# Two row tiles first, and later list rounds among the edge groups, in the head of a graph layer

## The chip, the core and the metric

The kernel runs on one core of one Trainium2 chip. The time is the device time of one execution in microseconds (us). The five engines of the core are called PE (matrix products and transposes), DVE (vector work), ACT (activations and copies), POOL (here it issues the indirect gathers) and SP (it issues the plain transfers). Each engine works through its own instructions in a fixed order; an instruction waits on semaphores for what it needs from others, and all that stands behind it on its engine waits too.

## The reference, cut to what matters

One layer takes `x` (6250 rows of 256 numbers), 200000 edges `src`, `dst` sorted by `dst`, and weights. It adds three parts: a graph attention, a linear attention over all rows, and a feed-forward part with four experts that is steered by a second, smaller graph attention over 131072 other edges.

```python
xn = _layernorm(x)
# graph attention, 4 heads of 64
z = jnp.einsum('ni,hid->nhd', xn, W)
es, ed = (z * a_src).sum(-1), (z * a_dst).sum(-1)
e = leaky(es[src] + ed[dst], 0.01)
alpha = softmax of e over the edges of one dst
gnn = segment_sum(alpha[:, :, None] * z[src], dst)
# linear attention over all rows
mix = layernorm_gamma(softmax(q) @ (softmax_over_rows(k).T @ v) @ Wout)
x = x + gnn + mix
x = x + ffn(_layernorm(x))      # a second attention over other edges picks experts
```

The change is in what stands ahead of the first attention's sums over edges: the first norm, `z`, the products with the two attention vectors, and the lists of edges.

## The kernel before

**Tiles.** The rows are cut into NT = 49 tiles of 128 (the last has 106). The first attention works on "chunks" of 128 edges of one destination tile: 33 chunks for each tile and 28 for the last, 1612 in all, taken in groups of G1 = 8.

**The head: project.** `load_x` (an SP transfer) brings XB = 7 tiles of x into one of three buffers `xa`. `project_x` treats such a batch: on DVE the statistics (`bn_stats`, `bn_aggr`, lines 519 and 520), on ACT a square root and on DVE five small steps that refine it (lines 125 to 135, called `ln_q`, `ln_r`); then for each tile the normalised rows `xn` (DVE, line 525), two transposes on PE into `ln_tp` (line 145), a copy to `xy` on ACT (line 529), two products `zp` on PE (line 532), and three copies out of `zp`: z to `zt` (ACT, line 534), the source term to the end of `zt` (DVE, line 537) and both terms to `es_all` (ACT, line 538). SP stores `zt` to the table `ztab` in memory (line 539). `zp` and `ln_tp` have two buffers each, `zt` has eight. The statistics of a batch are held back until the third tile of the batch before is normalised (`tc.issue_after`).

**The head: attention vectors.** `wz` holds the weights (256 columns) and eight more columns, the weights times the attention vectors (lines 576 and 577 on DVE, in four pairs of product and reduction). Since `zp` is a product with all 264 columns, these stand ahead of the first batch.

**The head: order of the edges.** A flag says whether `dst` is unsorted (`down`, `d`, `flag`, lines 590 to 597). Every engine reads it and branches (lines 599 to 602); the sorted data skip the branch. Behind it, lines 609 to 683 find where each destination tile begins in the sorted edges (`fd` in the room of `kx`, line 622; `lt`, `cf`, the product `cp`, `sel`, the product `row`, `less`, `start_k`, the product `ip`), and end with the addresses `at` (line 681). POOL then fetches with 26 indirect transfers (line 689) the sources `sr` and destinations `dr` of every chunk, two for each of BS = 13 blocks of 128 chunks.

**The head: lists.** `lists(b0)` makes four blocks ready for the edge stage: destinations less the tile's base (`fl`, line 700), clamped sources (`fs`, line 704), a bf16 copy (line 705) that SP stores as `rows_1` (line 706), then transposes on PE into `e_tp` (line 712) and copies on DVE to `src_c` and `dl_c` (line 713). `src_c` holds the row numbers that the edge stage gathers by. There are four rounds. Each is held back by `tc.issue_after` until a late tile is through: tiles NT - 17, NT - 10, NT - 3 and NT - 2.

```python
for b0, t in zip(range(0, BS, 4), (NT - 17, NT - 10, NT - 3, NT - 2)):
    with tc.issue_after(zmm[t].ins), tc.issue_after(xnv[t].ins), tc.issue_after(zst[t].ins):
        lists(b0)
```

`S.activation(warm, r[:, 0:1], AF.Exp)` reads the last batch's root; it is there to bring ACT's exponential table in.

**Behind the head.** Line 197 takes a maximum over `es_all` (`f_m`), then POOL begins the gathers of `ztab` by `src_c` (line 774), eight for each of 202 groups; three buffers `gt` hold them. A group's weights need the gathered source terms (`src_d`, line 208, ACT lines 209 and 210), destination terms (`ed`, line 813, from `pw3`) and one-hot matrices (lines 798 and 807); DVE weighs the rows (line 833) and PE adds them up (line 842). The linear attention's steps (`k_max` and others, whose running maximum is `kmax`, line 871) and the sort of the other edges are dealt out among the groups. A second edge stage of the same kind follows (line 1303 on POOL), with the experts' products beside it.

**What sets the order.** Instructions are not issued in the order of the text: a scheduler orders each engine's instructions when the program is built, by what it takes to be ready, within the data dependencies and the `issue_after` marks. A tile's buffer that takes the place of an older one waits for the older one's readers.

Of the kernel before, what the change touches and what calls it, by code (L numbers as in the profile page):

```python
# [9 lines left out]
F32 = mybir.dt.float32  # L10
# [10 lines left out]
P = 128  # L21
N = 6250
D = 256
# [33 lines left out]
def rows(t):  # L57
    return min(P, N - t * P)
# [3 lines left out]
def gps_layer(ctx: ExitStack, tc: tile.TileContext, a: dict, out: bass.AP):  # L62
# [425 lines left out]
    wz = room_2[:, : 2 * 264].rearrange("p (j f) -> p j f", j=2)  # L488
    es_all = room_2[:, 2 * 264 : 2 * 264 + NT * 8].rearrange("p (t f) -> p t f", f=8)
    XB = 7  # L490
    with tc.tile_pool(name="a_x", bufs=1) as ax, tc.tile_pool(name="a_w", bufs=3) as aw, tc.tile_pool(
        name="a_p", bufs=2, space=PSUM
    ) as aps:
# [5 lines left out]
        def load_x(t0):  # L499
            ts_ = range(t0, min(t0 + XB, NT))  # L500
            xa = aw.tile([P, XB, D], F32, name="xa")
            whole = [t for t in ts_ if rows(t) == P]
            SP.dma_start(
                xa[:, : len(whole)],
                a["x"][t0 * P : (t0 + len(whole)) * P, :].rearrange("(t p) d -> p t d", p=P),
            )
            for t in ts_:
                if rows(t) < P:
                    SP.dma_start(xa[: rows(t), t - t0], a["x"][t * P : N, :])
            xas[t0] = xa  # L510

        def project_x(t0):
            ts_ = range(t0, min(t0 + XB, NT))
# [8 lines left out]
            for t in ts_:  # L522
                n, n0 = rows(t), t * P
                xn = aw.tile([P, D], F32, name="xn")
                xnv[t] = V.tensor_scalar(
                    xn[:n], xa[:n, t - t0], mv[:n, t, 0:1], r[:n, t - t0 : t - t0 + 1], op0=OP.subtract, op1=OP.mult
                )
                tp = transposed(aps, xn, n, "ln_tp")
# [5 lines left out]
                S.copy(  # L534
                    zt[:n, :ZW].rearrange("p (h d) -> p h d", h=4)[:, :, 0:64], zp[:n, 0:256].rearrange("p (h d) -> p h d", h=4)
                )
                V.tensor_copy(zt[:n, ZW:], zp[:n, 256:260])
                S.copy(es_all[:n, t, :], zp[:n, 256:264])
                zst[t] = SP.dma_start(ztab[n0 : n0 + n, :], zt[:n])
            return r  # L540
# [20 lines left out]
        with tc.tile_pool(name="e_w", bufs=1) as w:  # L561
# [32 lines left out]
            with tc.tile_pool(name="fl_p", bufs=1, space=PSUM) as ps:  # L594
                d2 = ps.tile([1, 1], F32, name="d2")
                T.matmul(d2, d1, ones[:, 0:1], start=True, stop=True)
                V.tensor_scalar(flag, d2, 1.0, None, op0=OP.min)
            project_x(XB)
            unordered = nc.values_load(
                flag[0:1, 0:1], min_val=0, max_val=1, skip_runtime_bounds_check_because="a count of 0s and 1s, at most 1"  # L600
            )
# [1 line left out]
                with tc.tile_pool(name="ord_w", bufs=1) as ow:  # L603
                    order_edges(ow, bs, bd)

            load_x(3 * XB)
            project_x(2 * XB)
            for ord_, b_ in ((d_ord, bd), (s_ord, bs)):
                SP.dma_start(ord_.rearrange("(b r j) o -> r b (j o)", r=P, j=P), b_)
            with tc.tile_pool(name="e_l", bufs=1) as w, tc.tile_pool(name="e_p", bufs=1, space=PSUM) as ps:  # L610
# [68 lines left out]
                V.tensor_add(at_f, at_f, ip[:, :, 0])  # L679
                at = w.tile([P, BS], I32, name="at")  # L680
                V.tensor_scalar(at, at_f, float(B1 * P * P - P), None, op0=OP.min)
# [12 lines left out]
                fl = take(BS, P, F32)  # L694
                fb = tk.bitcast(BF16)[:, : BS * P].rearrange("p (b j) -> p b j", b=BS)

                def lists(b0):
                    bb = slice(b0, min(b0 + 4, BS))
                    nb = bb.stop - b0
                    V.tensor_tensor(  # L700
                        fl[:, bb], dr[:, bb], base[:, bb].unsqueeze(2).to_broadcast([P, nb, P]), op=OP.subtract
                    )

                    V.tensor_scalar(fs[:, bb], sr[:, bb], float(N - 1), None, op0=OP.min)
                    V.tensor_copy(fb[:, bb], fl[:, bb])
                    SP.dma_start(
                        rows_1[b0 * P * P : bb.stop * P * P, :].rearrange("(b s j) o -> s b (j o)", s=P, j=P), fb[:, bb]
                    )
                    for f, c_ in ((fs, src_c), (fl, dl_c)):
                        tp = ps.tile([P, 4, P], F32, name="e_tp")  # L710
                        for b in range(nb):
                            T.transpose(tp[:, b], f[:, b0 + b], ident)
                        V.tensor_copy(c_[:, b0 * P : (b0 + nb) * P], tp[:, :nb].rearrange("p b j -> p (b j)"))

                for t0 in range(3 * XB, NT, XB):
                    if t0 + XB < NT:
                        load_x(t0 + XB)
                    r = project_x(t0)
# [299 lines left out]
    with tc.tile_pool(name="g1_w", bufs=2) as w, tc.tile_pool(name="g1_g", bufs=3) as gp, tc.tile_pool(  # L1018
# [46 lines left out]
        for g in range(NGR):  # L1065
# [689 lines left out]
```

## Time and profile before

| what | before |
|---|---|
| median of 3 runs | 3260.65 us (3256.18 to 3268.05) |
| the profiled execution's own time | 3258.8 us |
| its span, first to last instruction | 3257.0 us |
| mean granted clock of PE | 0.857 |
| busy: PE, DVE, ACT, POOL | 2334.0, 2439.4, 480.6, 2344.4 us |
| `at` ready (line 681) | at 63.87 us |
| last tile's copy out of `zp` (line 537) | at 108.99 us |
| first gather of the edge stage (line 774) | at 114.90 us |
| last gather of that stage | at 2175.6 us |
| gathers of the second stage (line 1303) | 2200.4 to 3202.7 us |

Times in the trace are microseconds from the first instruction. A row of the timeline gives the start, the duration, the engine, the line, the operation, what it writes and reads, and in brackets how long the engine had been idle before it and what ended that. A name such as `src` or `dl` in a row is the buffer that a tile lies in, without its number: `wz` and `es_all` lie in `src_2`, so rows that write them say `src`; `lists` and `fd` work in the room of `kx`.

### The profile page before, as it was taken

To read this page: it belongs to the slowest core of one execution; us is meant where nothing else is said; L and a number is where in the kernel's file an instruction comes from. 1 tells how busy PE (TensorE), PEld (TensorE's weight loads), DVE (VectorE), ACT (ScalarE), POOL (GpSimd) and SP (SyncE) were. 2 spreads that over 40 slices of the span, in tenths; PEclk is the share of its full clock that TensorE was granted. 3 is DMA by queue.
4 is the path that set the end of the run, shared out by engine and by line. 5 is a ranking of instruction groups with operands and counts; after the bars stand their busy time and mean duration, and the time that the engine had idled before them with its cause. 6 is when DMAs were issued, how large, how long until landed. Compare 5 with 4: busy or idle time off the path is not lost. (4 is left out here: it accounts for less than half of the span.)

```text
span 3257.0 us, 36396 instructions
## 1 busy us (share of the span) xinstructions
PE 2334.0 (72%) x10899; PEld 1699.4 (52%) x10900; DVE 2439.4 (75%) x6337; ACT 480.6 (15%) x1266; POOL 2344.4 (72%) x2436
## 2 busy tenths in 40 slices
PE   7677778865666574665665666658777877888888
PEld 5555666654455453554544545445455545555555
DVE  7587767788888887886886878667676766777775
ACT  3200111111111111111111111013111111111111
POOL 2577777777777777777777777757777777777772
PEclk9788888987888887787888878779998998999989
DMA  6544444445555555555555555534223223333321
GB/s 202 155 135 135 136 129 127 137 134 145 150 139 151 143 137 140 138 141 143 141 153 142 147 140 142 138 92 101 61 62 78 60 57 92 81 76 80 78 51 37
DMA packets 248273, 384.90 MB, mean 118 GB/s; under 512 B 73414, under 2 KB 156246, under 8 KB 248057
## 3 DMA queue, kind: packets, MB, share of 16 engines
q0 software_dynamic: 103296, 230.96, 28.9%
q1 hardware_dynamic: 142857, 150.87, 15.4%
q8 instruction: 91, 1.49, 0.2%
q14 instruction: 125, 1.02, 0.1%
q10 hardware_dynamic: 1904, 0.56, 0.1%
HBM read 345.44 MB, written 36.74 MB: 117 GB/s over the span
## 5 line engine op out<-in xcount | busy, mean ns | idle before, releaser
L774 POOL DMA_INDIRECT gt<-ztab,src_c x1612 | 1551.2, 962 | 528.1 <-issue 424.7
L842 PE MATMUL ag<-gt,oh 128*128 128x260 f32 x3224 | 980.1, 461 | 348.3 <-DVE gt L833 347.0
L842 PEld LDWEIGHTS ag<-gt,oh 128*128 128x128 f32 x3224 | 732.6, 234 | 516.0 <-DVE gt L833 375.9
L1303 POOL DMA_INDIRECT gt<-htab,src x784 | 764.6, 975 | 262.5 <-issue 210.0
L833 DVE TENSOR_TENSOR gt<-gt,dv 128x1040 f32<-128x1040 f32 x403 | 488.8, 1223 | 0.2 <-DVE src L409 0.2
L1424 PE MATMUL yo<-w,hT 128*128 128x256 f32 x1568 | 420.8, 411 | 15.8 <-DVE ys L1467 15.8
L1404 PE MATMUL hp<-xy,w 128*128 128x512 f32 (+1 forms) x832 | 407.2, 612 | 8.6 <-ACT hT L1409 4.5
L1424 PEld LDWEIGHTS yo<-w,hT 128*128 128x128 f32 x1568 | 303.5, 203 | 96.1 <-issue 26.3
L208 DVE TENSOR_TENSOR src_d<-gt,most 128x32 f32<-128x32 f32 x204 | 38.6, 189 | 355.6 <-DMA gt<-ztab,src_c 344.3
L868 PE MATMUL m<-wqkv,xy 128*128 128x256 f32 (+1 forms) x784 | 235.8, 436 | 88.8 <-DVE kmax L879 43.6
L798 DVE TENSOR_TENSOR oh<-dv,dl_c 128x1024 f32<-128x1024 f32 x202 | 243.9, 1207 | 0.0
L868 PEld LDWEIGHTS m<-wqkv,xy 128*128 128x128 f32 (+1 forms) x784 | 160.7, 215 | 125.1 <-DVE kmax L879 49.6
L1404 PEld LDWEIGHTS hp<-xy,w 128*128 128x128 f32 x832 | 159.9, 205 | 112.4 <-issue 98.3
L1409 ACT ACTIVATE hT<-hp,b 128x512 f32<-128x512 f32 (+1 forms) x208 | 132.8, 660 | 517.6 <-PE hp L1404 294.9
L209 ACT ACTIVATE src_f<-src_d,shift_c 128x32 f32<-128x32 f32 x202 | 64.9, 321 | 928.2 <-DVE src_d L208 836.3
L1361 DVE TENSOR_TENSOR pr<-dv,gt 128x64 f32<-128x64 f32 x98 | 21.9, 223 | 227.0 <-DMA gt<-htab,src 219.5
L1385 PE MATMUL ag<-mq,oh 128*128 128x120 bf16 x784 | 66.3, 236 | 150.4 <-DVE mq L1377 141.0
L813 PE MATMUL ed<-pw,ohT 128*128 128x24 bf16 x1612 | 72.1, 175 | 125.5 <-DVE ohT L807 111.1
L373 DVE MAX8 src<-dl 128x8 f32<-128x1024 f32 x128 | 156.0, 1219 | 0.4 <-issue 0.4
L1385 PEld LDWEIGHTS <-oh 128*128 128x128 bf16 x784 | 51.6, 107 | 198.5 <-DVE mq L1377 176.6
L375 DVE MATCH_REPLACE8 dl<-src,dl 128x1024 f32<-128x1024 f32 x127 | 153.4, 1208 | 0.0
L813 PEld LDWEIGHTS <-ohT 128*128 128x128 bf16 x1612 | 64.0, 98 | 165.4 <-DVE ohT L807 134.3
(350 smaller groups left out, 2695.0 us busy)
## 6 DMA issues: line engine op xcount, KB each, us to landing
br<-rows SPq DMA_DIRECT2D x299, 256.0 KB
gt<-ztab,src_c POOLq DMA_INDIRECT x1612
gt<-htab,src POOLq DMA_INDIRECT x784
early<-ys SPq DMA_DIRECT2D x24, 512.0 KB
ys<-early SPq DMA_DIRECT2D x24, 512.0 KB
ztab<-zt SPq DMA_DIRECT2D x48, 132.0 KB
row<-in_x_dram SPq DMA_DIRECT2D x48, 128.0 KB
out_dram<-ys SPq DMA_DIRECT2D x48, 128.0 KB
```

Source lines behind the costliest of these rows:

```text
L373: V.max(out=srtf[:, 8 * i : 8 * i + 8], in_=keyf)
L375: V.match_replace(out=keyf, in_to_replace=srtf[:, 8 * i : 8 * i + 8], in_values=keyf, imm_value=0.0)
L774: G.indirect_dma_start(out=self.gt[:, c, :], out_offset=None, in_=ztab[:, :], in_offset=bass.IndirectOffsetOnAxis(ap=self.idx[:, c : c + 1 ...
L798: V.tensor_tensor(self.oh[:, :n], self.dv[:, None, :P].to_broadcast([P, n, P]), self.dl[:, :, None].to_broadcast([P, n, P]), op=OP.is_equal,)
L813: T.matmul(self.ed[:, c, :], self.ohT[:, c * P : (c + 1) * P], pw3[:, ds(self.tiles[c], 1), :].rearrange("p a b -> p (a b)"), start=True, ...
L833: V.tensor_mul(gz, gz, self.wp[:, c0:c1].unsqueeze(3).to_broadcast([P, c1 - c0, 4, 65]))
L842: T.matmul(sums[t], self.oh[:, c], self.gt[:, c, 0:ZW], start=(s0 + c == 0 or chunk_tile[s0 + c - 1] != t), stop=last,)
L868: T.matmul(out_, xy[:, t, j, :n], wqkv[:, j, c0 : c0 + D], start=(j == 0), stop=(j == 1))
L1303: G.indirect_dma_start(out=self.gt[:, c, : tab.shape[1]], out_offset=None, in_=tab[:, :], in_offset=bass.IndirectOffsetOnAxis(ap=self.idx[ ...
L1404: T.matmul(hp[:, :m], wts[e][0][:, c, j * P : (j + 1) * P], xy[:, t0 : t0 + nt, c] if m == nt * P else xy[:, t0, c, :m], start=(c == 0), s ...
L1409: S.activation(h[:, :m], hp[:, :m], AF.Gelu, bias=b1[:, e, j : j + 1])
L1424: T.matmul(yo[:n], hT[j][:, o : o + n], wts[e][1][:, j, :], start=(j == 0 and e < EARLY), stop=(j == 3))
```

## The change

The first seven tiles become two batches, of two and of five tiles; the 42 others stay in batches of seven. The two first loads go out together ahead of the others. The products with the attention vectors stand behind the normalised rows of the first two tiles, and are done for both halves of the weights at once: two products and two reductions of twice the size. The load of a later batch is asked for one batch ahead, as before. `base` moves to a pool that lives through the edge stage. Only round 0 of `lists` stays in the head; rounds 1, 2 and 3 are called in the edge loop after groups 2, 6 and 10, with `e_tp` in the edge stage's own psum pool (one buffer), and without `issue_after` marks. `warm` reads the constant `eps`.

```diff
+    batches = [range(0, 2), range(2, XB)] + [range(t0, min(t0 + XB, NT)) for t0 in range(XB, NT, XB)]
...
-        def project_x(t0):
-            ts_ = range(t0, min(t0 + XB, NT))
-            xa = xas[t0]
-            with tc.issue_after(xnv[t0 - XB + 2].ins) if t0 else nullcontext():
+        def project_x(i, weights=None):
+            ts_, t0 = batches[i], batches[i][0]
+            xa = xas[i]
+            with tc.issue_after(xnv[batches[i - 1][0] + min(2, len(batches[i - 1]) - 1)].ins) if i else nullcontext():
...
+            ready = {}
+            if weights:
+                ready = {t: normal(t) for t in ts_}
+                weights()
+            for t in ts_:
+                n, n0 = rows(t), t * P
+                xn = ready[t] if weights else normal(t)
...
         load_x(0)
+        load_x(1)
...
-            load_x(XB)
             load_blocks(bs, a["src"], E1)
-            load_x(2 * XB)
-            for s in range(2):
-                for j in range(2):
-                    V.tensor_mul(prs[:, j], wz[:, j, 0:256], avs[:, s])
+            load_x(2)
+
+            def weights():
+                for s in range(2):
+                    V.tensor_mul(prs, wz[:, :, 0:256], avs[:, None, s].to_broadcast([P, 2, D]))
                     V.tensor_reduce(
-                        wz[:, j, 256 + 4 * s : 260 + 4 * s], prs[:, j].rearrange("p (h d) -> p h d", h=4), AX.X, OP.add
+                        wz[:, :, 256 + 4 * s : 260 + 4 * s], prs.rearrange("p j (h d) -> p j h d", h=4), AX.X, OP.add
                     )
-            project_x(0)
-            with tc.issue_after(xnv[2].ins):
+
+            project_x(0, weights)
+            load_x(3)
+            project_x(1)
+            with tc.issue_after(xnv[4].ins):
...
-            project_x(XB)
+            project_x(2)
...
-            load_x(3 * XB)
-            project_x(2 * XB)
+            load_x(4)
+            project_x(3)
...
-                base = w.tile([P, BS], F32, name="base")
+                base = ek.tile([P, BS], F32, name="base")
...
-                def lists(b0):
+                def lists(ps, b0):
...
-                        tp = ps.tile([P, 4, P], F32, name="e_tp")
+                        tp = ps.tile([P, 4, P], F32, name="e_tp", bufs=1)
...
-                S.activation(warm, r[:, 0:1], AF.Exp)
-
-                for b0, t in zip(range(0, BS, 4), (NT - 17, NT - 10, NT - 3, NT - 2)):
-                    with tc.issue_after(zmm[t].ins), tc.issue_after(xnv[t].ins), tc.issue_after(zst[t].ins):
-                        lists(b0)
+                S.activation(warm, eps, AF.Exp)
+
+                with tc.issue_after(zmm[NT - 17].ins), tc.issue_after(xnv[NT - 17].ins), tc.issue_after(zst[NT - 17].ins):
+                    lists(ps, 0)
...
             sorted_ = upto_
+            if g % 4 == 2 and g // 4 + 1 < (BS + 3) // 4:
+                lists(ps, 4 * (g // 4 + 1))
```

More of the change, by code (lines that the diff above doesn't have):

```diff
@@ L497, in gps_layer, with load_x @@
         xas, xnv, zmm, zst = {}, {}, {}, {}
-        def load_x(t0):
-            ts_ = range(t0, min(t0 + XB, NT))
+        def load_x(i):
+            ts_, t0 = batches[i], batches[i][0]
             xa = aw.tile([P, XB, D], F32, name="xa")
@@ L509, in load_x @@
                     SP.dma_start(xa[: rows(t), t - t0], a["x"][t * P : N, :])
-            xas[t0] = xa
-        def project_x(t0):
-            ts_ = range(t0, min(t0 + XB, NT))
-            xa = xas[t0]
-            with tc.issue_after(xnv[t0 - XB + 2].ins) if t0 else nullcontext():
+            xas[i] = xa
+        def project_x(i, weights=None):
+            ts_, t0 = batches[i], batches[i][0]
+            xa = xas[i]
+            with tc.issue_after(xnv[batches[i - 1][0] + min(2, len(batches[i - 1]) - 1)].ins) if i else nullcontext():
                 for t in ts_:
@@ L521, in project_x, with normal @@
             r = rstd_of(aw, mv[:, t0 : t0 + len(ts_), 1], P, len(ts_), "ln")
-            for t in ts_:
-                n, n0 = rows(t), t * P
+            def normal(t):
+                n = rows(t)
                 xn = aw.tile([P, D], F32, name="xn")
@@ L527, in project_x @@
                 )
+                return xn
+            ready = {}
[5 more added lines that the diff above has]
+                xn = ready[t] if weights else normal(t)
                 tp = transposed(aps, xn, n, "ln_tp")
@@ L539, in project_x @@
                 zst[t] = SP.dma_start(ztab[n0 : n0 + n, :], zt[:n])
-            return r
         avs, prs = q_2[:, : 2 * D].rearrange("p (s d) -> p s d", s=2), q_2[:, 2 * D :].rearrange("p (s d) -> p s d", s=2)
@@ L713, in lists @@
                         V.tensor_copy(c_[:, b0 * P : (b0 + nb) * P], tp[:, :nb].rearrange("p b j -> p (b j)"))
[L715 to L718, printed above, removed]
-                S.activation(warm, r[:, 0:1], AF.Exp)
-                for b0, t in zip(range(0, BS, 4), (NT - 17, NT - 10, NT - 3, NT - 2)):
-                    with tc.issue_after(zmm[t].ins), tc.issue_after(xnv[t].ins), tc.issue_after(zst[t].ins):
-                        lists(b0)
+                for i in range(4, len(batches)):
+                    if i + 1 < len(batches):
+                        load_x(i + 1)
+                    project_x(i)
+                S.activation(warm, eps, AF.Exp)
+                with tc.issue_after(zmm[NT - 17].ins), tc.issue_after(xnv[NT - 17].ins), tc.issue_after(zst[NT - 17].ins):
+                    lists(ps, 0)
                 T.transpose(row[0:1, :NX], start_k[:NX], ident[:NX, :NX])
```

## The prediction

> **What bounds the kernel now.** I read the page's table of the costliest groups first, then the waits between 95 and 125 us, then the timeline of the head, engine by engine. In both kernels I also read the order in which the built program issues its instructions on each engine; that order is fixed, and for the kernel before it agrees row for row with the timeline.
>
> ```profile
> L774 POOL DMA_INDIRECT gt<-ztab,src_c x1612 | 1551.2, 962 | 528.1 <-issue 424.7
> ```
> ```profile
> POOL gt L774 <- PE mx_t L187: 17.6, 1, 17.6
> ```
> ```profile
> 114.90 0.94 POOL L774 DMA_INDIRECT gt<-ztab,src_c  x1 [17.65 <-PE mx_t L187]
> 116.15 0.95 POOL L774 DMA_INDIRECT gt<-ztab,src_c  x1 [0.31 <-issue]
> ```
>
> After the head, POOL gathers rows one chunk every 1.25 us (0.95 busy, 0.30 of its own issue): 1612 of them need 2015 us at that pace and took 2061 (the last starts at 2175.6). So the edge stage runs at POOL's pace, and what the change can move is the start of the first gather. That start follows the last tile of z:
>
> ```profile
> 33.53 2.30 DVE L525 TENSOR_SCALAR xn<-xa,mv,ln_r 128x256 f32<-128x256 f32 x3 [3.06 <-DVEq L602]
> 39.64 0.99 DVE L622 CAST kx<-bd 128x1664 f32<-128x1664 int32 x1
> 63.87 0.17 DVE L681 TENSOR_SCALAR at<-at_f 128x13 int32<-128x13 f32 x1
> 79.29 0.15 DVE L537 COPY zt<-zp 128x4 f32<-128x4 f32 x1
> 95.06 0.72 DVE L700 TENSOR_TENSOR kx<-kx,base 128x512 f32<-128x512 int32 x1 [0.58 <-DMA kx<-d_ord,at]
> 98.06 0.43 DVE L704 TENSOR_SCALAR kx<-kx 128x512 f32<-128x512 int32 x1 [2.28 <-DMA kx<-s_ord,at]
> 98.74 0.15 DVE L537 COPY zt<-zp 128x4 f32<-128x4 f32 x1
> 108.99 0.16 DVE L537 COPY zt<-zp 106x4 f32<-106x4 f32 x1 [1.28 <-ACT zt L534]
> 111.61 0.29 DVE L713 CAST src_c<-e_tp 128x128 int32<-128x128 f32 x1 [0.42 <-PE e_tp L712]
> 113.96 0.50 DVE L197 TENSOR_REDUCE f_m<-src 128x4 f32<-128x196 f32 x1 [2.05 <-DMA gamma<-in_L_mix_gamma_dram]
> ```
>
> The reader is to see: (1) `at`, the addresses of the 26 list gathers, is ready at 63.87, just after tile 20's copy; (2) DVE stands still for 2.9 us up to 98.06, between tiles 40 and 41, because the lists' third round waits for those gathers; (3) tile 48, the last, is copied at 108.99; (4) the list copies behind it are over at 111.9, before the wait for the last stores ends at 113.96. Their removal from this place gains nothing.
>
> **The change part by part.** Let T be the time of `at`.
>
> *Start.* The weights on DVE run from 9.17 to 11.83, four products and four reductions of 256. Two products of 512 at 0.69 (row L700 has this size) and two reductions of about 0.66 (estimate, from 0.37 for 256) also give 2.7: nothing. With two tiles' statistics ahead of them, the first xn moves from 17.08 to 9.17 + 2.7 + four small steps of 0.2 = 12.7, 4.4 us earlier, but for two tiles only. The five others follow with 1.0 of constants, 0.7 of two xn, 2.3 of statistics, a table load and the root (1.6), then 1.2 of refinement between copies that wait for cold products: their xn starts at 19.3, where tile 2 had it at 17.8. DVE does the same work before the branch at L602 less two xn (0.7 us); it reached the branch at 30.47 and does so at about 30.2. Value taken: 0, bounds -2 and +2.
>
> *After the branch.* The order has turned. Before, DVE had two normalised tiles in stock there and came to the cast of bd at 39.64. In the changed kernel the cast comes at once (33.5), and PE's first instruction is the count product cp, ahead of tile 7. PE is idle from about 28 to 37.5. Tile 7's xn comes after the chain that took 5.5 us in the kernel before (39.64 to 45.19): 33.5 + 5.5 = 39.0. Up to T, PE then has tiles 7 to 18: two at cold products (3.5 + 0.8), ten at 1.33 (two tiles' products took 2.05, transposes 0.3 each), the row products (0.64 + 0.86 + 0.86 + 1.29 = 3.65) and ip (3.45): 39.4 + 4.3 + 13.3 + 3.65 + 3.45, and 0.5 for the copies: T = 64.6, say 65. DVE's own sum (18 xn of 0.33, 17 statistics of 0.45, 5 us of list work, 3.5 of copies and refinement) ends near 62. So T comes 1.1 later, bounds -2 and +5: the gain of the start is used up.
>
> *The lists.* The text puts three rounds among the edge groups, but only their transposes and copies go there. The arithmetic (L714, L718, L719) is no longer held behind late tiles, and in the built order it stands early in the head: round 1 after tile 30 (before: after tile 36), the rest after tile 36, behind a memset of kmax that waits for all 26 gathers. These take T + 0.46 + 1.279 k for number k (64.33 to 96.31 for 25 steps) and land 1.75 after they start (96.31 to 98.06).
> - Round 1: tile 30's copy comes at T + 15.4 (79.29), DVE is free at T + 16.3, number 14 lands at T + 20.1. Stall 3.8, and tile 32 comes at T + 22.6 where it was at T + 18.1. Behind the waiting DVE are the copies that free zp, so PE stands too.
> - kmax: four more tiles at 1.53 bring T + 29; DVE's own 7 us say T + 29.6. Number 25 lands at T + 34.2. Stall 4.6, where the kernel before lost 2.9.
> - Then ten tiles' products are left. In the kernel before, six took from 99.15 to about 108.4 after its stall (groups of PE at 99.15, 104.58 and 107.37, the last 1.14 long): 1.53 each. T + 35 + 15.3 + 0.5 = T + 50.8 for the last copy, against T + 45.1.
>
> Last copy: 65 + 50.8 = 115.8, 6.8 us later than 108.99. The stores and the maximum behind it take 5.9 as before (108.99 to 114.90); the first gather starts at 121.7.
>
> *The clock.* The window 100 to 105 has a granted clock of 0.66 after the stall, and products of 1.7 us per tile. [...] By the row my two runs are 6.1 + 15.3 us. [...] I take the row.
>
> *The table.* `warm` now depends on a constant, and the built order has it right after the first root: exponential table in, root table back in, and the exponential again at L217. The table load on line 719 shows 1.28 with the next activation right behind it. [...] I take the row.
>
> *In the edge stage.* Three copies of 0.68 stand in DVE's order before group 0 is weighed. POOL meets group 0 only when gather 24 wants its buffer, at 145.09; PE had done with it at 140.25. A delay under 4.8 us costs nothing, and I expect 2 to 3. Without that cover each microsecond over it would be lost once. The later copies, in the groups around 10, lie beside gathers. SP's list stores move with the arithmetic and pass no load of x; PE's order of the steady groups is the same.
>
> Sum: 0 + 1.1 + 5.7 + 0 = +6.8. The profiled execution (3258.8, span 3257.0) becomes 3265.6. It stands 1.85 below the median of the runs, 3260.65; the same step on the median gives 3267.
>
> **The rivals.**
> *The head gets shorter as the words say.* If tiles 0 and 1 carry their 4.4 us to T, and POOL's gathers with it, the stall of 2.9 may vanish too: 3260.65 - 4 to - 9 = 3252 to 3257. For it: PE does start earlier. Against it: cp heads PE's queue after the branch, and the waits are in the order.
> *A long stall.* PE stands behind cp, and the clock falls; if T slips to 75 instead of 65, all behind it slips: +17 us, 3278. It decides from T = 74.5 on (0.5% is 16.3 us). Against it: DVE's own sum of 62; for it: DVE and PE wait for each other with two zp buffers, and every stall adds a cold stretch.
> *Moved copies break the gather pace.* If group 0 is delayed by 8 us, 3 us are lost at gather 24; with the head's shift 3270.
>
> **How the numbers follow.** About 0.5%, or 16 us, is what a measurement of this kernel can tell from no change. Later by 1 to 14 us: 0.68, time 3267. Shorter head: 0.14. Long stall: 0.14, of which nearly all lies beyond 16 us. Broken pace: 0.04. For faster by over 16 us the head would have to lose a seventh of itself: 0.03 for what I do not see. Slower 0.14, within 0.83. The range takes the shorter head to -6 and the long stall to about +18: 3254 to 3279.
>
> **What would show it.** In the changed profile: the first xn near 12.7, but `at` at 63 to 67; a DVE wait for the s_ord or d_ord gathers near tile 31, and a second of 3 to 6 us ahead of the kmax memset; the last zt copy near 116; the first gather near 122; from there a step of 1.25 without gaps at gather 24. An `at` below 60, or a first gather below 115, proves the main case wrong; a gap in POOL after gather 24 proves the cover wrong.

## The result, and the profile after

The changed kernel takes 3278.53 us (median of 6 runs, 3275.48 to 3284.61); the kernel before, in the same sitting, 3266.51 (median of 6, 3256.18 to 3268.66). The ratio is 1.0047, interval 1.0034 to 1.0059: 12 us by the medians, slower. The prediction had +6.8, and took anything under 16 us for a step that can't be told from no change; this one of 12 us is told. The direction and the two stalls were right, the size was not. The profiled executions are 19.7 us apart (3258.8 and 3278.5), but the one of before lies 8 us below its own median.

Ten of the 18 experiment runs fell into sittings in which every kernel, the one before too, took about 3950 to 4030 us by the medians, and the first gather came at 135 to 145 us; of those only what lies ahead of `at`, at about 70 us, is read here.

First the page and POOL's timeline of the kernel after: the group of gathers, then single gathers (start, duration, then in brackets the idle time and what ended it).

```profile
L787 POOL DMA_INDIRECT gt<-ztab,src_c x1612 | 1555.2, 965 | 536.7 <-issue 423.8
```
```profile
126.20 0.94 POOL L787 DMA_INDIRECT gt<-ztab,src_c  x1 [22.29 <-DVE f_m L197]
...
155.64 0.95 POOL L787 DMA_INDIRECT gt<-ztab,src_c  x1 [0.30 <-issue]
158.55 0.94 POOL L787 DMA_INDIRECT gt<-ztab,src_c  x1 [1.96 <-PE ed L826]
```

The first gather moved from 114.90 to 126.20, +11.3 us, and gather 24 (158.55) shows a gap that the kernel before had not: 1.96 us idle instead of 0.30. POOL's pace between gathers is unchanged (1.251 us, median step of both traces). So the head is longer, and a little is lost once behind it: the first 24 gathers take 2.2 us more. From the first gather to the last it takes 2068.7 us, and 2060.7 before. The other 6 us of this difference are not put down to the change: the same length is 2060.5 in `held`, 2065.3 in `head_only_3`, whose lists are the old ones, and 2071.4 in `branch_late_2` (kernels described below). The head on DVE's timeline, after:

```profile
37.30 0.18 DVE L521 BATCH_NORM_AGGREGATE mv<-st 128x2 f32<-128x6 f32 x1 [6.39 <-DVEq L616]
37.53 1.03 DVE L636 CAST kx<-bd 128x1664 f32<-128x1664 int32 x1
...
70.64 0.18 DVE L695 TENSOR_SCALAR at<-at_f 128x13 int32<-128x13 f32 x1
...
91.41 0.77 DVE L714 TENSOR_TENSOR kx<-kx,base 128x512 f32<-128x512 int32 x1 [4.33 <-DMA kx<-d_ord,at]
...
105.89 0.27 DVE L884 MEMSET kmax<- 128x256 f32 x1 [3.96 <-DMA kx<-s_ord,at]
...
120.85 0.16 DVE L548 COPY zt<-zp 106x4 f32<-106x4 f32 x1 [0.72 <-ACT zt L545]
125.47 0.50 DVE L197 TENSOR_REDUCE f_m<-src 128x4 f32<-128x196 f32 x1 [4.46 <-DMA ztab<-zt]
```

Each line answers to one of before. The wait at the branch (`DVEq L616`) is 6.39 us where it was 3.06. The cast of bd comes at 37.53 (forecast 33.5). `at` comes at 70.64 (65 forecast, 63.87 before). The two stalls stand where they were forecast, at `at` + 20.8 and ending at `at` + 35.25, and are 4.33 and 3.96 us long (3.8 and 4.6); before, the memset of kmax stands at 100.37, behind the lists' third round, and waits for nothing. The last zt copy is at `at` + 50.2 (50.8).

What happened at the branch is seen in SP's timeline (the load of x for tiles 21 to 27, before and then after), in the windows (busy time of PE, PE's weight loads, DVE, ACT and POOL, each with its count, then PE's clock, the DMA share and GB/s) and in the DMA queues of single microseconds, 34 to 35 and 35 to 36, of the kernel after:

```profile
24.21 0.38 SPq L503 DMA_DIRECT2D xa<-in_x_dram  x1
```
```profile
30.44 0.43 SPq L504 DMA_DIRECT2D xa<-in_x_dram  x1
```
```profile
30.00:32.00 2.00, 0.00 (x0) 0.00 (x0) 0.91 (x6) 0.17 (x1) 0.00 (x0) 0.62 0.37 74
32.00:34.00 2.00, 0.00 (x0) 0.00 (x0) 0.00 (x0) 0.00 (x0) 0.00 (x0) 0.50 0.79 255
34.00:36.00 2.00, 0.00 (x0) 0.00 (x0) 0.00 (x0) 0.00 (x0) 0.00 (x0) 0.50 0.58 205
36.00:38.00 2.00, 0.00 (x0) 0.00 (x0) 0.65 (x2) 0.30 (x1) 0.41 (x3) 0.50 0.02 4
```
```profile
q1 hardware_dynamic: 354, 0.36, 100.6%
q14 instruction: 1, 0.01, 2.2%
```
```profile
q1 hardware_dynamic: 46, 0.04, 10.8%
q14 instruction: 1, 0.01, 2.4%
```

From 32 to 36 us all five engines stand while one transfer runs: this load, 896 KB, issued by SP at 30.44 as the last thing ahead of its own load of the flag. Instruction packets (q14) come near the end of it, and the engines go on 1 to 2 us later. In the kernel before this transfer was issued at 24.21 and was through by 31.

### The profile page after: what moved, and what is told of

Read it like the earlier page. It is cut to its first block, busy times and chain, and to the rows that moved or that the text cites. A ratio compares the mean times of both kernels' runs of the same rounds, so it can differ in the third digit from the quotient of the medians.

```text
span 3276.4 us, 36402 instructions
## 1 busy us (share of the span) xinstructions
PE 2333.7 (71%) x10899; PEld 1699.0 (52%) x10900; DVE 2441.9 (75%) x6338; ACT 483.4 (15%) x1269; POOL 2349.8 (72%) x2436
## 3 DMA queue, kind: packets, MB, share of 16 engines
q0 software_dynamic: 103296, 230.96, 30.2%
## 5 line engine op out<-in xcount | busy, mean ns | idle before, releaser
L826 PE MATMUL ed<-pw,ohT 128*128 128x24 bf16 x1612 | 72.9, 175 | 133.3 <-DVE ohT L820 124.9
```

The lines of the kernel that those rows point to most:

```text
L826: T.matmul(self.ed[:, c, :], self.ohT[:, c * P : (c + 1) * P], pw3[:, ds(self.tiles[c], 1), :].rearrange("p a b -> p (a b)"), start=True, ...
```

## The experiments

The numbers that decide, from the other runs (`at` and first gather from one profile of each kernel, the gather from POOL's row; "rest" is the median less the first gather; some expectations give a first gather 0.1 to 0.2 us earlier than its row):

| kernel | `at` | first gather | median | ratio to before, interval | rest |
|---|---|---|---|---|---|
| before | 63.9 | 114.9 | 3262.8 to 3266.5 (four sittings) | | 3148 to 3152 |
| changed | 70.6 | 126.2 | 3278.5 | 1.0047 (1.0034 to 1.0059) | 3152 |
| head_only_3 | 69.7 | 115.6 | 3267.1 | 1.0010 (1.0001 to 1.0019) | 3151 |
| held | 70.1 | 128.7 | 3278.1 | 1.0056 (1.0036 to 1.0076) | 3149 |
| memsets_held | 70.3 | 124.0 | 3277.9 | 1.0038 (1.0026 to 1.0050) | 3154 |
| both_held | 71.1 | 119.0 | 3270.8 | 1.0015 (1.0008 to 1.0022) | 3152 |
| both_held_late | 68.9 | 117.7 | 3267.4 | 1.0008 (0.9999 to 1.0018) | 3150 |
| held_before | 65.5 | 124.9 | 3275.1 | 1.0033 (1.0022 to 1.0044) | 3150 |
| both_held_before | 62.9 | 111.0 | 3264.6 | 1.0003 (0.9994 to 1.0012) | 3154 |
| branch_late_2 | 61.7 | 112.7 | 3263.4 | 1.0000 (0.9991 to 1.0009) | 3151 |

The rest is 3148 to 3154 in all of them: the time follows the first gather, give or take 3 us.

**Each part alone: lists_only, head_only and their repeats.**

```
lists_only: before + base in ek, lists(ps, b0), e_tp bufs=1, round 0 at tile NT-17,
            lists(ps, 4 * (g // 4 + 1)) in groups g = 2, 6, 10
head_only:  changed kernel - those, with
            for b0, t in zip(range(0, BS, 4), (NT - 17, NT - 10, NT - 3, NT - 2)): ... lists(b0)
```

> The kernel before with the lists part of the change alone: rounds 1 to 3 of the lists stand in the edge groups, the first batch is still seven tiles behind the weights. Theory (each part has its own cost): the branch takes about 3 us as in the kernel before and `at` comes near 64, but DVE waits about 4 us for the gathers of round 1 and about 4 us at the memset of kmax, so the last zt copy is 50 us after `at`, near 114, the first gather near 120 (before: 114.9), and 1 to 2 us go at the gathers from 24 on. Time about 6 to 8 us above the kernel before, near 3273. Rival (the stalls cost only because the head part had delayed `at`): first gather within 1.5 us of 114.9, time within 2 us of the kernel before.

> The changed kernel with the lists as they were before: four rounds behind tiles NT-17, NT-10, NT-3, NT-2. Theory: the wait at the branch stays near 6.4 us and `at` near 70.6 (before: 63.9); from `at` to the first gather it takes 51 us as before, so the first gather comes near 121.5 and no gap is left at gather 24. Time about 6 to 7 us above the kernel before, near 3273. Rival (the head part is free by itself, `at` does not set the pace): first gather below 117, time within 2 us of the kernel before.

Both are among the ten runs of which only the start is read, and so are three repeats, `lists_only_2`, `lists_only_3` and `head_only_2`:

> The head part of the change alone (first batch of two tiles, lists in four rounds as before), once more, as in the run `head_only` transfers and tiles behind `at` were delayed in both kernels alike. Theory: the branch takes about 6 us and `at` comes near 70.5; the lists' third round then waits for gathers that end near 102, the first gather comes near 121, 6 us after the kernel before's 114.9. Time 5 to 7 us above the kernel before. Rival (the lists part causes all of the loss): first gather within 2 us of 114.9, time within 2 us of the kernel before.

> The lists part of the change alone (first batch of seven, rounds 1 to 3 in the edge groups), once more for the same reason. Theory: `at` near 63.5, the memset of kmax (or round 1) waits for the gathers until about 98, the last zt copy comes near 114 and the first gather near 119.5, 4 to 5 us after the kernel before's, and 1 to 2 us go at the gathers from 24 on: time 5 to 7 us above the kernel before. With head_only_2 the two parts then add up to the changed kernel's 11 to 14. Rival (the stalls only cost together with a late `at`): first gather within 1.5 us of 114.9.

> The lists part of the change alone (first batch of seven, rounds 1 to 3 in the edge groups), since in both runs before it everything behind `at` was slowed in the kernel before too. After head_only_3 (first gather 115.4) the theory is that the lists part makes the whole loss, because its memsets of kmax and y_mv tie the last tiles to the last list gather: first gather 55 us after `at`, as in the changed kernel, so near 118.5 with `at` near 63, and 1 to 2 us at the gathers from 24 on; time 4 to 6 us above the kernel before. The rest of the changed kernel's 11 us then comes of the later `at` (70.6), which costs nothing by itself. Rival (the lists cost the whole 11 us by themselves): first gather near 125, time 11 to 14 us above the kernel before.

What their start says is the same each time. Lists alone: the wait at the branch is 2.9 us and `at` at 62.1 to 62.8, as before. Head alone: 5.8 and 5.7 us at the branch and `at` at 70.0 and 71.0. So branch and `at` belong to the head part. The head part alone could be read to its end once:

> The head part of the change alone, once more, since in both runs before it everything behind `at` was slowed in the kernel before too. Expected as there: `at` near 70.5 and the first gather near 121, 6 us after the kernel before's, time 5 to 7 us above it. Rival (the lists part causes all of the loss): first gather within 2 us of 114.9, time within 2 us of the kernel before.

`at` is at 69.71, as expected, but the first gather is at 115.59, not 121; the time is 3 us (0 to 6) above the kernel before. DVE's timeline of head_only_3:

```profile
69.71 0.18 DVE L695 TENSOR_SCALAR at<-at_f 128x13 int32<-128x13 f32 x1
...
105.77 0.29 DVE L714 TENSOR_TENSOR kx<-kx,base 128x128 f32<-128x128 int32 x1 [1.79 <-DMA kx<-d_ord,at]
...
106.35 0.27 DVE L885 MEMSET kmax<- 128x256 f32 x1
...
110.11 0.16 DVE L548 COPY zt<-zp 106x4 f32<-106x4 f32 x1 [0.73 <-ACT zt L545]
```

The last list gathers come as late as in the changed kernel, at `at` + 36. But here the instructions that wait for them stand behind late tiles (NT - 3 and NT - 2), and only 4 zt copies follow the last wait. In the changed kernel 12 follow the memset at 105.89, and these take 1.34 us each (106.08 to 120.85). A late `at` costs little by itself; it costs when tiles are queued behind what waits for its gathers. (This profile also had a granted clock of 1.00 from 70 to 74 us, the changed kernel 0.68; such a fall is worth 2 to 3 us, see the end.) The expectation of 6 us fell: with the old list rounds a later `at` does not pass on to the end in full. What the lists alone cost on the head of before was not measured. By the prediction's own count, `at` + 50.2 for the last copy and 5.35 behind it, an `at` of 63.9 would give a first gather near 119.5; that is an estimate. Nearest to it is `held_before` below, with the lists moved and one wait at a memset: 124.9.

**The branch: load_late.**

```
-            load_x(4)
-            project_x(3)
             for ord_, b_ in ((d_ord, bd), (s_ord, bs)):
-                SP.dma_start(...)
+                stored = SP.dma_start(...)
+            with tc.issue_after(stored.ins):
+                load_x(4)
+            project_x(3)
```

> The changed kernel with one transfer moved: the load of x for tiles 21 to 27 is issued behind the stores d_ord and s_ord, so behind the branch, where it was the last transfer ahead of the branch's load of the flag. Theory (the engines stand at the branch until this 896 KB transfer is through, because what they need for it comes over the same DMA engines): the wait at the branch falls from 6.4 us to about 3.1, the cast of bd comes near 34, `at` near 67.4, the first gather near 123 (126.2 in the changed kernel). Time about 3 us below the changed kernel. Rival (the branch waits for another engine, or takes 6 us for its own sake): the wait stays near 6.4 us, `at` near 70.6, time as the changed kernel or up to 2 us more, as x of tiles 21 to 27 comes later.

DVE's timeline of load_late:

```profile
33.82 0.18 DVE L521 BATCH_NORM_AGGREGATE mv<-st 128x2 f32<-128x6 f32 x1 [3.45 <-DVEq L616]
34.05 1.03 DVE L637 CAST kx<-bd 128x1664 f32<-128x1664 int32 x1
```

The wait is 3.45 us, the cast at 34.05 and `at` at 67.4, each as the theory had it; what follows `at` is not read here. With the same edit both_held_late waits 3.72 us where both_held waits 5.98. So the transfer ahead of the branch makes 2.3 to 2.9 us of the wait. The theory's reason, that what the engines need comes over the same DMA engines, was not shown by itself: in the changed kernel one q14 packet moved from 34 to 35 us and one from 35 to 36, beside the end of the transfer, and the engines stood until it had ended. Which step of the branch waits was not isolated.

**The stalls: marks, held, memsets_held, both_held.**

```
marks:        with tc.issue_after(xnv[NT - 1].ins):      V.memset(kmax, -3e38)
              with tc.issue_after(head_end.ins):         lists(ps, 4 * (g // 4 + 1))
held:         kmax as in marks;
              with tc.issue_after(now.weighed.ins):      lists(ps, 4 * (g // 4 + 1))
memsets_held: with tc.issue_after(xnv[NT - 1].ins):      V.memset(kmax, -3e38); V.memset(mv, 1.0)
both_held:    the memsets as in memsets_held, the lists as in held
```

> The changed kernel with two issue_after marks: list rounds 1 to 3 may not be issued on DVE ahead of the end of the head (head_end), and the memset of kmax not ahead of the last tile's xn. Theory (DVE's two waits for the list gathers, 4.3 and 4.0 us, stand in the chain of tiles): no wait for s_ord or d_ord gathers in DVE beyond round 0, the last zt copy about 42 us after `at` instead of 50, near 112.5, the first gather near 118 (126.2), and some of it lost again if the later list work delays group 0: 0 to 4 us at gather 24. Time 4 to 8 us below the changed kernel. Rival (the stalls are covered, PE's clock or ACT sets the pace of the tiles): last copy still 48 to 50 us after `at`, first gather near 125, time within 2 us of the changed kernel.

In `V.memset(mv, 1.0)` the tile is the one that rows call y_mv. `marks` is one of the ten and tells only that `at` stayed at 70.9. `held` put the same question once more:

> The changed kernel with the later list work held back on DVE: the memset of kmax may not be issued ahead of the last tile's xn, and round r of the lists not ahead of the last weighing of its edge group (2, 6, 10). Theory (DVE's two waits for the list gathers, 4.3 and 4.0 us in the changed kernel, stand in the chain of tiles): `at` near 70.6 as in the changed kernel, no DVE wait for list gathers behind round 0, the last zt copy about 42 us after `at` instead of 50, the first gather near 118 (126.2), no gap at gather 24. Time about 10 us below the changed kernel, near the kernel before. Rival (PE or ACT sets the pace of the tiles and the waits are covered): last copy still 48 to 50 us after `at`, first gather near 125, time within 2 us of the changed kernel.

The expectation fell: first gather 128.7, later than in the changed kernel. DVE's timeline of held:

```profile
105.04 0.14 DVE L886 MEMSET y_mv<- 128x98 f32 x1 [12.39 <-DMA kx<-s_ord,at]
```

A second memset, of y_mv, lies beside that of kmax and waits for the same gathers. With round 1 no longer in front of it, it took the whole wait at once: 12.39 us, ending at `at` + 35 as the wait of the kmax memset did, and again with 12 zt copies behind it. So with a memset in this place, round 1's stall of 4.33 us costs nothing: it only uses up part of the wait that ends there anyway. (Held is even 2.5 us later; PE comes out of the longer wait at a granted clock of 0.50 from 100 to 110, where the changed kernel has 1.00.)

> The changed kernel with the two memsets (kmax and y_mv) held behind the last tile's xn, the list rounds left where they are. Theory (round 3's arithmetic is next in line for the last list gathers, so it takes the place of the memset): a DVE wait of 4 us near `at` + 20 and another that ends near `at` + 34, the first gather near 126 and a time within 2 us of the changed kernel. Rival (the memsets alone make the second wait): no second wait, first gather near 120, time about 6 us below the changed kernel.

DVE's timeline of memsets_held, round 1's wait and the last one for a gather:

```profile
91.81 0.69 DVE L714 TENSOR_TENSOR kx<-kx,base 128x512 f32<-128x512 int32 x1 [5.06 <-DMA kx<-d_ord,at]
...
105.62 0.23 DVE L718 TENSOR_SCALAR kx<-kx 128x128 f32<-128x128 int32 x1 [0.73 <-DMA kx<-s_ord,at]
```

Taking away the memsets alone gives 2.2 us at the first gather (124.0) and nothing in the time. The theory was right on the time and wrong on the waits. Round 1's grew from 4.33 to 5.06 us, but rounds 2 and 3 wait less than 1 us in all for their gathers, the last until 105.62 (`at` + 35.3), with 10 copies behind it. The rival was half right. Gather 24 shows a gap here too, 1.26 us idle. Both together then:

> As `held`, and the memset of y_mv, which stands beside that of kmax and also waits for the last of the 26 list gathers (12.4 us of DVE in `held`), is held behind the last tile's xn too. Theory (whatever DVE instruction stands first in line for the gathers holds the tiles until `at` + 35; only with all of them moved does the stall go): no DVE wait over 1 us for list gathers, last zt copy between 108.5 and 111, first gather between 114 and 117 (128.5 in `held`, 126.2 in the changed kernel, 114.9 in the kernel before), so about 11 us below the changed kernel and within 2 us of the kernel before. Rival (the tiles after `at` + 35 would come at that time anyway, as ACT or the stores of zt hold them): first gather above 122, time within 4 us of the changed kernel.

DVE's and POOL's timelines of both_held:

```profile
109.70 0.27 DVE L885 MEMSET kmax<- 128x256 f32 x1 [2.81 <-DMA ztab<-zt]
...
113.46 0.16 DVE L548 COPY zt<-zp 106x4 f32<-106x4 f32 x1 [0.73 <-ACT zt L545]
```
```profile
119.04 0.95 POOL L787 DMA_INDIRECT gt<-ztab,src_c  x1 [14.71 <-PE mx_t L187]
```

Ahead of the last tile's xn no wait over 1 us for list gathers is left on DVE. Behind it one wait remains: the memset of kmax stands for 2.81 us. The profile puts this wait to a store of zt, but the same memset in both_held_before waits for the last list gather by its row (3.69 us, below); that it is this gather here too was not shown. Only 4 zt copies follow it, so it costs 1 to 2 us (an estimate, from the 2.83 us that two tiles take here). If it is the gather, "no DVE wait over 1 us for list gathers" was missed. The first gather is at 119.04: 7.2 us earlier than in the changed kernel, 9.6 earlier than in held, and 5.0 earlier than in memsets_held, which is about the 5.06 us of round 1's stall, though the wait at the memset and the clock (below) are in that difference too. So without the memsets that stall counts, for about its length. The time is 7.7 us below the changed kernel's median (of another sitting; against before, 1.0015 instead of 1.0047). The gap at gather 24 is gone as well: 30.6 us from the first gather to number 24, 32.4 in the changed kernel, 30.2 before. I had expected 114 to 117. The windows (columns as above) of both_held and of held behind `ip`, from 70 to 74, show where 2 to 3 us of the rest went:

```profile
70.00:74.00 4.00, 4.00 (x12) 3.30 (x12) 2.08 (x12) 0.54 (x2) 2.05 (x2) 0.50 0.07 18
```
```profile
70.00:74.00 4.00, 3.66 (x18) 2.92 (x18) 3.88 (x22) 1.73 (x7) 2.87 (x3) 1.00 0.29 74
```

The same products ran at half clock in the one profile and at full clock in the other: eight products of `zp` took 3.89 us instead of 2.05.

**The same on the old head, and the parts together: held_before, both_held_before, both_held_late.**

```
held_before, both_held_before: lists_only + the marks of held, of both_held
both_held_late:                load_late + the marks of both_held
```

> The kernel before (first batch of seven tiles, weights ahead of it) with list rounds 1 to 3 in the edge groups, held back on DVE behind the last weighing of groups 2, 6 and 10, and the memset of kmax behind the last tile's xn. Theory: `at` near 63, the 2.9 us that DVE lost to the third round are gone, the last zt copy near 105.5 and the first gather near 111 (before: 114.9), so 3 to 4 us below the kernel before. Rival (the copies of the lists in the edge groups cost POOL's pace): a gap of 2 us or more behind gather 24 or in groups 2 to 11, and the time at or above that of the kernel before.

> As `held_before` (the kernel before with list rounds 1 to 3 held back into edge groups 2, 6 and 10), with the memset of y_mv held back as well as that of kmax. Theory: no DVE wait over 1 us for list gathers, the last zt copy near 105.5, the first gather near 111 (before: 114.9), time 3 to 5 us below the kernel before. Rival (list work in the edge groups costs POOL's pace): a gap of 2 us or more among the first 100 gathers and a time at or above that of the kernel before.

> `both_held` and the late transfer of `load_late` together: the load of x for tiles 21 to 27 behind the branch. Theory (the two costs add): branch wait near 3.3 us, `at` near 67.4, first gather near 112.5, 2 to 3 us below both_held and 1 to 3 us below the kernel before. Rival (tiles 21 to 27 then wait for their x): `at` near 67.4, but a DVE wait for x behind tile 20 and a first gather no earlier than in both_held.

DVE's timelines of held_before and of both_held_before:

```profile
101.09 0.14 DVE L872 MEMSET y_mv<- 128x98 f32 x1 [11.37 <-DMA kx<-s_ord,at]
```
```profile
101.56 0.27 DVE L871 MEMSET kmax<- 128x256 f32 x1 [3.69 <-DMA kx<-s_ord,at]
```

On the old head the place of the wait for the gathers moves the first gather from 111.0 (both_held_before) to 124.9 (held_before), and the time by 10.5 us (medians of two sittings; `at` differs by 2.6). The expectation of held_before fell as that of held did, by the same y_mv memset (11.37 us, 12 zt copies behind it). both_held_before still waits 3.69 us at the memset of kmax (both_held_late 3.81), where the theory had no wait over 1 us; but only 4 copies stand behind it. Its first gather is where the theory put it, 3.9 us earlier than before, but the time is not shorter (1.0003, 0.9994 to 1.0012). No gap among the first 100 gathers explains that: they take 127.5 us, 127.3 before. From its first gather to its last it takes 2066.5 us, 2060.7 before, a length that varies as much between profiles of kernels with the old lists (2065.3 in head_only_3). Its first gather is from one profile, and the rest varies by 3 us between kernels, so where the 4 us went stays open. both_held_late against both_held gains 1.3 us at the first gather and 3.4 by the medians, the direction and about the size expected, but the first gather is 117.7 and not 112.5, and the kernel is no faster than before.

**PE's empty queue behind the branch: branch_late, head_branch_late.**

```
both_held_late, and
+            with tc.issue_after(xnv[8].ins):
                 unordered = nc.values_load(...)
head_branch_late: head_only with the edits of load_late and branch_late
```

> `both_held_late` with the load of the flag, and so the branch, held behind tile 8's xn on DVE. What the head part still costs there (first gather 117.6, with 110.9 in both_held_before) is put down to PE, which has no normalised tile in stock behind the branch and stands from 28 to 41 us. Theory: with tiles 7 and 8 normalised ahead of the branch, as tiles were in the kernel before, PE's gap around the branch shrinks from 13 us to 4 or less; `at` may come up to 2 us later, which nothing waits for any more; the first gather comes near 112.5, 5 us earlier than in both_held_late. Time about 4 us below both_held_late, 2 to 3 below the kernel before. Rival (`at` still sets the pace, or the tiles are late for another reason): first gather at 116 or later, time within 2 us of both_held_late.

> branch_late once more, since in the first run everything behind `at` was slowed in the kernel before too. From that run `at` is at 60.4 and PE's gap around the branch 3.7 us. Theory: with the lists' waits gone the head now ends by the pace of the tiles, 2 us ahead of both_held_before, whose `at` is at 62.9: first gather between 107 and 111, and a time 4 to 7 us below the kernel before. Rival (the last tiles are held by something else, such as the gathers or the stores): first gather near 113 or later, time within 2 us of both_held_late, 2 to 3 us above the kernel before.

> The head part with the lists in four rounds as before, the load of x for tiles 21 to 27 behind the branch, and the branch behind tile 8's xn on DVE (as in branch_late). Theory: `at` near 61.5, no tile waits for the list gathers for more than 2 us, since they end near 95; the first gather between 108 and 112 (head_only_3: 115.4, before: 114.9), time 2 to 6 us below the kernel before. Rival (the tiles' own pace, ACT and PE, ends the head): first gather near 113 to 115, time within 2 us of the kernel before.

In the changed kernel no tile was normalised ahead when the branch came. PE's timelines, the kernel after and then branch_late_2:

```profile
28.08 1.16 PE L543 MATMUL zp<-src,xy 128*128 128x264 f32 x4 [0.41 <-ACT src L549]
42.26 0.64 PE L652 MATMUL cp<-cf,ones 128*128 128x48 f32 x2 [13.02 <-DVE ln_q L134]
```
```profile
27.90 1.16 PE L543 MATMUL zp<-src,xy 128*128 128x264 f32 x4 [0.41 <-ACT src L549]
32.75 1.11 PE L145 MATMUL ln_tp<-ident,xn 128*128 128x128 f32 x4 [3.69 <-DVE xn L527]
```

PE's gap shrinks from 13.02 to 3.69 us (the same in branch_late), and `at` comes at 61.7 (branch_late_2), 60.4 (branch_late) and 60.2 (head_branch_late), ahead of the kernel before. So the head part's late `at` comes of this gap and the x transfer. The first gather of branch_late_2 is at 112.7: 5 us earlier than both_held_late, as expected from that comparison, but later than the 107 to 111 expected in its second run, and the time is that of the kernel before (1.0000, 0.9991 to 1.0009). Its first gather is 1.7 later than both_held_before's, although `at` is 1.2 earlier: with few tiles behind the waits, `at` no longer sets the end. head_branch_late is one of the ten, so whether two tiles first gains anything with the old lists stays open.

**The kernel before once more: before_again.**

> The kernel before, unchanged, for a second profile of it. If the first gather's time is a property of the kernel, it comes within 1.5 us of 114.9, `at` within 1.5 of 63.9. If the profiled execution shown first was a short one in its edge stage (it lies 6 us below the median of the later runs), the 1612 gathers now take 2063 to 2068 us from first to last instead of 2060.7; if they take 2061 again, the 2063 to 2068 us of the kernels with lists in the edge groups are a cost of those lists.

It is one of the ten: `at` at 62.4 and 2.9 us at the branch agree with the first profile, but the length of its edge stage can't be compared.

## Why the prediction missed the size

*Start.* First xn at 12.15 (12.7 forecast), tile 2's at 19.48 (19.3). Right. DVE reached the branch at 30.9 (30.2).

*After the branch: the step that failed.* "The cast comes at once (33.5)" took the branch's wait from the trace of before, 3.06 us, as a constant. It was 6.39, because the head part had moved a transfer of 896 KB up against it; the order of SP's queue showed this transfer ahead of the flag, and I did not price it (load_late: 3.45 us with this transfer moved). That made the cast 4.0 us late (0.7 for reaching the branch later, 3.3 for the wait). From the cast to `at` it took 33.1 us and not 31.5: PE's timeline has 56 products of `zp` there, 14 tiles (7 to 20), and I had counted twelve; the two more are 2.7 us at 1.33 each, and shorter terms gave some back (`ip` 3.02 for 3.45, the row products 3.42 for 3.65). Together `at` came 5.6 us later than forecast: +6.8 against before where I had +1.1, beyond my bound of +5.

*The lists.* Both stalls, their places and the last copy at `at` + 50.8 were right (50.2). The account of them was only half right. They are not two costs of 3.8 and 4.6 us to be added: with round 1's stall gone the wait at the memset ends at the same `at` + 35 (held). The end is `at` + 35 and 12 zt copies, whatever waits in between. And that is why the later `at` counted in full, where with the old lists it hardly did (head_only_3).

*The tail.* 5.35 us from the last copy to the first gather, 5.9 forecast.

*The cover at gather 24.* I gave group 0's delay 2 to 3 us under a cover of 4.8. The sums of group 0 began 26.3 us behind the first gather (152.49), 20.5 before (135.40), so 5.8 later, and gather 24 lost 1.66 us over its usual 0.30. In DVE's and PE's timelines of the kernel after, a list copy waits behind DVE's `src_d`, and PE's transposes wait for the one buffer `e_tp`, ahead of group 0's terms `ed`:

```profile
141.15 0.19 DVE L208 TENSOR_TENSOR src_d<-gt,most 128x32 f32<-128x32 f32 x1 [6.78 <-DMA gt<-ztab,src_c]
141.25 0.68 DVE L727 COPY dl_c<-e_tp 128x512 f32<-128x512 f32 x1
```
```profile
141.99 1.12 PE L726 MATMUL e_tp<-ident,kx 128*128 128x128 f32 x4 [6.92 <-DVE dl_c L727]
...
146.13 0.41 PE L826 MATMUL ed<-pw,ohT 128*128 128x24 bf16 x8
```

I had counted the copies, and neither the transposes behind them nor the single buffer. In held and both_held, where the rounds stand behind a group's weighing, the gap is gone.

The sum over again: 6.8 + 5.6 (`at`) - 0.6 (last copy) - 0.5 (tail) gives +11.3 at the first gather, as measured, and 1.7 at gather 24 makes 13, against 12 by the medians.

*The noise.* I took 16 us for the least that can be told. The interval, 0.34% to 0.59%, tells 12 us. That the measured 3278.5 lies inside the range of 3254 to 3279 is luck in part: the kernel before was itself 6 us slower in this sitting than the median the range was built on.

*The rivals.* The head did not get shorter. The long stall gave a better number (3278) but not the mechanism: it needed `at` beyond 74.5, through DVE and PE waiting for each other. Broken pace did happen, with 1.7 us of its 3.

## What to carry over

When a change moves a transfer, look at what stands behind it in its queue, the branch included: a wait copied from the trace of before is not a constant (3.06 us before, 6.39 in the changed kernel). When several instructions in one queue wait for the same run of late events, their waits overlap: an earlier one only uses up part of a later one (4.33 and 3.96 us in the changed kernel, the second until `at` + 35.25; one wait of 12.39 in held, until `at` + 35). Count what is queued behind the last of them, here 12 tiles at 1.34 us (4 in head_only_3), rather than adding up the waits; and look for the next in line, which took over the wait when one of the waiters was held back. Lateness of a value costs by what is queued behind its users: with `at` 6 us later and 4 tiles behind the last wait, the time was 3 us (0 to 6) longer.

## What the hardware showed that I had not expected

In the changed kernel all five engines stood at the branch until a plain transfer of 896 KB had ended (32 to 36 us). DVE waited 5.7 to 6.4 us in the kernels that issue it last ahead of the flag's load, 2.9 to 3.7 us in the others. A flag and a branch thus cost DVE about 3 us here even with no such transfer ahead; these rows show the whole stop, not its parts.

PE was busy without a gap through the 26 narrow products `ip` (48x2 each; 3.79 us in both_held, 3.02 in the others named here), and yet the granted clock behind them, from 70 to 74 us, was 0.50 in both_held, 0.65 in memsets_held and 0.68 in the changed kernel, but 1.00 in held and head_only_3, whose instructions there are the same. The rows show no idle time there, and no run here tests what brings the fall; the cause stays open. It moves single profiles by 2 to 3 us (both_held against held: 2.1 behind `at`, 0.8 in `ip`).
